# Last stage of a two-layer decoder: half tiles of 64 rows with up to two experts, expert weights laid out anew in DRAM

## The chip, the cores and the metric

The kernel runs on one NeuronCore of one Trainium2 chip. The metric is device time in microseconds, the median of three runs. TensorE (PE) multiplies matrices, VectorE (DVE), ScalarE (ACT) and GpSimd (POOL) do elementwise work, and DMA transfers are issued by SyncE (SP), ACT or POOL, each in its own order. All data are 32-bit floats.

## The reference, cut to what matters

The input x is 8 sequences of 256 tokens of 256 values, 2048 tokens in all. Two decoder layers follow each other, each with three parts that are added to x: layer 0 has self-attention, attention over a given memory `ctx_2048` and a feed-forward part with Sinkhorn routing; layer 1 has self-attention, attention over the same memory with one null key in front, and a mixture of eight experts, of which each token takes one, beside a shared expert that all tokens take. That last part is what the change is about (a = all 2048 tokens, D = 256, F = 704, E = 8; x is the layer-normed input):

```python
def _L1_ffn_ref(x_bsD, router_DE, w1_eDF, w3_eDF, w2_eFD, ws1_DF, ws3_DF, ws2_FD):
    x_aD = x_bsD.reshape(a, d)
    scores_aE = x_aD @ router_DE
    vals_aK, idx_aK = jax.lax.top_k(scores_aE, 1)
    masked_aE = jnp.full_like(scores_aE, -jnp.inf).at[jnp.arange(a)[:, None], idx_aK].set(vals_aK)
    gates_Ea = jax.nn.sigmoid(masked_aE).T
    routed_in_EaD = gates_Ea[:, :, None] * x_aD[None, :, :]
    mid_EaF = jax.nn.silu(einsum('ead,edf->eaf', routed_in_EaD, w1_eDF)) * einsum('ead,edf->eaf', routed_in_EaD, w3_eDF)
    routed_out_EaD = jnp.einsum('eaf,efd->ead', mid_EaF, w2_eFD)
    shared_aD = jax.nn.silu(x_aD @ ws1_DF) * (x_aD @ ws3_DF) @ ws2_FD
    out_aD = shared_aD + routed_out_EaD.sum(axis=0)
```

An expert's output for a token that did not choose it is zero, so the kernel computes each token with its own expert only.

## The kernel before, in words

`decoder` (L56) calls `plain` (L67), the usual path, and then tests `odd_i`: only where a check on the data failed does `general` compute everything again (L61 to L64). `plain` runs its stages in this order. Times are from the profiled execution.

- **Units of attention, 0 to about 600 us.** A loop (L739) goes over the units: self-attention of layer 0 and attention over the memory, two per sequence, then self-attention of layer 1. Each unit's `load()` is called two units ahead (L748); the memory keys and values (`memk` L424, `memv` L426) are loaded there on SP. At the second turn `expert_tables` (L491) prepares tables for layer 0's experts; it also fills the DRAM buffers `xs` and the end of `ys` with zeros, by DMAs from POOL (L496, L497). Layer 0's experts are woven in between.
- **The attention with a null key, about 600 to 1150 us** (`null_cross_attention`, L860), with two quarters of the shared expert at its end. `hidden` (L818) is the first half of a SwiGLU expert, `silu(x w1) * (x w3)`, for any number of columns; a `quarter` is `hidden` for 512 tokens.
- **The last stage, `token_experts` (L1072).** DVE works out from the router's scores which expert each token takes and its place in a list sorted by expert in which each expert begins at a new tile of 128 rows (L1117 to L1175), and which expert each tile has, `exp_i` (L1186). POOL scatters the 2048 scaled rows to these places in the DRAM buffer `xs`, in 16 indirect DMAs (L1195). Meanwhile TensorE does further shared work (`quarter(2)`, `joined`). Then come the tiles, `slots(0, 19)` (L1259, called at L1274), with an order of TensorE's instructions that is written out by hand: while tile t + 1 goes through `into`, tile t waits to go through `outof`, and tile t + 2 is `fetched`.
  - `fetched` (L1229), all on SP: the tile's 128 rows from `xs` into `xr` (four buffers; this DMA waits for all 16 scatters), a register load of the tile's expert, two DMAs for w1 and w3 side by side (`w_in`, L785, three buffers, and a copy of a tail of 64 columns by POOL, L790), two for w2 (`w_out`, L798). Then TensorE transposes the rows (L1243) and ACT copies them out of PSUM (L1245).
  - `into` (L1248): `hidden` for 128 rows, 22 matrix products written in the code, which the profile shows as 44 records `h` (L825); ACT does SiLU (L830), DVE the product (L831).
  - `outof` (L1254): six products written in the code, twelve records `out` (L1093), a copy by ACT (L1256) and a DMA by ACT's queue into `ye` (`ys` in the profile, L1257).
  - The list has room for 23 tiles. Registers of all engines load the number of filled tiles, and tiles 19 to 22 run only if it is above 19 (L1275 to L1279).
  - Then `quarter(3)` (L1285), 16 gathers by POOL from `ye` back to token order (L1288), DVE's additions, `joined(3)` and the output DMAs on SP (L1295 to L1302).

`product` splits a matrix product in two, each for 64 of the 128 rows of its output, which run side by side in the two halves of the array; the profile marks them 128*64, whole ones 128*128:

```python
def product(out, lhsT, rhs, start, stop):
    for h in (slice(0, 64), slice(64, P)):
        nc.tensor.matmul(out[h], lhsT[:, h], rhs, start=start, stop=stop, skip_group_check=True)
```

Outside the hand-written orders, a scheduler places each engine's instructions, DMA issues included, by when their inputs are ready and by program order.

Of the kernel before, what the change touches and what calls it, by code (L numbers as in the profile page):

```python
# [38 lines left out]
P = 128  # L39
# [11 lines left out]
SLOTS = NT + E - 1  # L51
NEG = -1.0e30
# [14 lines left out]
def plain(ctx: ExitStack, tc: tile.TileContext, a: dict, out: bass.AP, odd_i: bass.AP):  # L67
# [69 lines left out]

    xs = dram.tile([SLOTS * P, D], F32, name="xs")
    ye = dram.tile([SLOTS * P, D], F32, name="ys")

# [190 lines left out]
    class SelfAttention:  # L331
# [5 lines left out]
        def load(self):  # L337
            if self.layer == 0 and self.b > 1:
                load_x(self.b)

# [150 lines left out]
    def expert_tables():  # L491
# [4 lines left out]
        nc.gpsimd.dma_start(xs.rearrange("(s p) d -> p s d", p=P), zero.unsqueeze(1).to_broadcast([P, SLOTS, D]))  # L496
        nc.gpsimd.dma_start(  # L497
            ye[19 * P :].rearrange("(s p) d -> p s d", p=P), zero.unsqueeze(1).to_broadcast([P, SLOTS - 19, D])
        )

# [148 lines left out]
    def weights_x():  # L649
# [3 lines left out]
        ctxs = ctx.enter_context(tc.tile_pool(name="ctxs", bufs=2, side="right"))  # L653
        wproj = ExitStack()
        wp = wproj.enter_context(tc.tile_pool(name="wp", bufs=1, side="right"))
# [117 lines left out]
    fit = const.tile([P, B], F32, name="fit")  # L773

    w_l0.close()

# [41 lines left out]
    def hidden(mid, w13, cols, pair, silu):  # L818

        n = cols.shape[2]  # L820
        for i in range(NFC):
            h1, h3 = pair(n)
            for h, lo in ((h1, i * P), (h3, FF + tail + i * P))[: 2 if i < full else 1]:
                for c in range(2):
                    nc.tensor.matmul(h, w13[:, c, lo : lo + P], cols[:, c, :], start=c == 0, stop=c == 1)  # L825
            fw = P
            if i == full:
                fw, h1, h3 = tail, h1[:tail], h1[tail:]
            sl = silu(n)[:fw]
            nc.scalar.activation(sl, h1, AF.Silu)  # L830
            yield nc.vector.tensor_tensor(mid[:fw, i, :n], sl, h3, ALU.mult)  # L831

# [27 lines left out]
    def null_cross_attention(phase):  # L860
# [129 lines left out]

        def divide(oT, rs):
# [29 lines left out]
        def quarter(q):  # L1021
            return hidden(shared["mid_s"][q], shared["ws13"], shared["xnT"][:, :, bass.ts(q, 2 * S)], pair, silu)
# [8 lines left out]
        for b in range(B):  # L1031
# [13 lines left out]
            rs, old = reciprocals(b, den, en), en  # L1045
            if more:
# [25 lines left out]
    def token_experts(phase):  # L1072
        one = phase.enter_context(tc.tile_pool(name="e1", bufs=1))
        work = phase.enter_context(tc.tile_pool(name="e2", bufs=2))
        wts = phase.enter_context(tc.tile_pool(name="e3", bufs=3))
# [3 lines left out]
        xnT, ws13, ws2, mid_s = (shared[n] for n in ("xnT", "ws13", "ws2", "mid_s"))  # L1079

        mid_r = [ended(one.tile([P, NFC, P], F32, name=f"midr{i}")) for i in range(2)]
        w2_r = [ended(one.tile([P, NFC, D], F32, name=f"w2{i}")) for i in range(3)]
# [14 lines left out]
        def quarter(q):  # L1097
            mid = mid_s[q % 2]
            for last in hidden(mid, ws13, xnT[:, :, bass.ts(q, 512)], pair, silu):
                pass  # L1100
            return mid, last
# [8 lines left out]
        def row(n, step, name):  # L1110
            i = one.tile([P, n], I32, name=f"{name}_i")
            nc.gpsimd.iota(i, [[step, n]], base=0, channel_multiplier=0)
# [3 lines left out]

        ecol, tcol, jcol = row(E, -1, "ecol"), row(SLOTS, 1, "tcol"), row(NT, P, "jcol")  # L1117
        nc.vector.tensor_scalar(ecol, ecol, float(E), None, ALU.add)
# [28 lines left out]
        for j in range(NT):  # L1147
            nc.vector.tensor_tensor(run[:, j + 1, :], run[:, j, :], count[:, j, :], ALU.add)
        over = one.tile([P, E, NT], F32, name="overe")
        nc.vector.tensor_tensor(  # L1150
            over,
            run[:, NT, :].unsqueeze(2).to_broadcast([P, E, NT]),
            jcol.unsqueeze(1).to_broadcast([P, E, NT]),
            ALU.is_gt,
        )
        tiles = one.tile([P, E], F32, name="tiles")
        nc.vector.tensor_reduce(tiles, over, AX.X, ALU.add)
        at = one.tile([P, E + 1], F32, name="at")
        nc.vector.memset(at[:, 0:1], 0.0)
        for e in range(E):  # L1160
            nc.vector.tensor_tensor(at[:, e + 1 : e + 2], at[:, e : e + 1], tiles[:, e : e + 1], ALU.add)
        filled_i = one.tile([P, 1], I32, name="filled_i")
        nc.vector.tensor_copy(filled_i, at[:, E : E + 1])
        rows = one.tile([P, E], F32, name="rowse")
        nc.vector.tensor_scalar(rows, at[:, :E], float(P), None, ALU.mult)
        nc.vector.tensor_tensor(run[:, :NT, :], run[:, :NT, :], before, ALU.add)
        nc.vector.tensor_tensor(
            run[:, :NT, :], run[:, :NT, :], rows.unsqueeze(1).to_broadcast([P, NT, E]), ALU.add
        )
        nc.vector.tensor_tensor(run[:, :NT, :], run[:, :NT, :], hot, ALU.mult)  # L1170
        pos = one.tile([P, NT], F32, name="pos")
        nc.vector.tensor_reduce(pos, run[:, :NT, :], AX.X, ALU.add)
        nc.vector.tensor_scalar(pos, pos, SLOTS * P - 1.0, None, ALU.min)
        pos_i = one.tile([P, NT], I32, name="pos_i")
        nc.vector.tensor_copy(pos_i, pos)  # L1175
        past = one.tile([P, SLOTS, E - 1], F32, name="past")
        nc.vector.tensor_tensor(
            past,
            tcol.unsqueeze(2).to_broadcast([P, SLOTS, E - 1]),
            at[:, 1:E].unsqueeze(1).to_broadcast([P, SLOTS, E - 1]),  # L1180
            ALU.is_ge,
        )
        exp_f = one.tile([P, SLOTS], F32, name="exp_f")
        nc.vector.tensor_reduce(exp_f, past, AX.X, ALU.add)
        exp_i = one.tile([P, SLOTS], I32, name="exp_i")
# [20 lines left out]
        for q in range(3):  # L1206
# [6 lines left out]
            alld = dens.rearrange("p k t h -> p (k t h)")  # L1213
        inside = one.tile([P, 3 * NT * H], F32, name="inside")
# [1029 lines left out]
```

## Time and profile before

| | |
|---|---|
| median of three runs | 1417.25 us (1415.31 to 1417.82) |
| the profiled execution | 1415.5 us, its span 1413.4 us |
| TensorE busy | 1371.9 us, 97% of the span |
| DVE, ACT, POOL busy | 499.1, 461.9, 386.2 us |
| DMA over the span | 91.23 MB, mean 65 GB/s |
| granted clock of TensorE | 0.993 of full speed on average |
| the 19 tiles | 1226.55 to 1374.07 us |
| the test for further tiles, until TensorE goes on | 1374.07 to 1376.02 us |
| `quarter(3)` and `joined(3)` on TensorE | 1376.02 to 1405.5 us |
| last output DMA issued | 1406.57 us |

A line of the profile names the line of the code, the engine, the operation, the tiles it writes and reads, the form of a product in the array (rows * columns in use), partitions by elements, and the number of records, then busy time, the mean duration of one in ns, and the idle time of the engine just before, with what ended it. Products are pipelined: a record's duration is longer than the distance to the next one, so costs are read from start to start. In a timeline a line is a run of equal instructions: its start, its length, what it is. PEclk is the clock granted to TensorE, in parts of full speed. "DMA share" is the mean busy share of the 16 DMA engines.

### The profile page before, as it was taken

How to read it: one execution, taken by the hardware profiler on the slowest of the kernel's cores; microseconds unless marked ns; L12 is line 12 of the kernel's file. 1: busy time of each engine (PE TensorE's matmuls, PEld its weight loads, DVE VectorE, ACT ScalarE, POOL GpSimd, SP SyncE). 2: the span in 40 equal slices, each digit the busy share in tenths (PEclk: the TensorE clock that was granted, in tenths of full speed). 3: DMA queues.
4: the chain of work that ended last, by engine and by line, in shares of the span. 5: the costliest groups of instructions: out<-in, count | busy, mean ns of one | idle time of the engine just before them, and what ended most of it. 6: DMA issues, size and time to landing. Idle time of an engine off the chain costs nothing. (4 is left out here: it accounts for less than half of the span.)

```text
span 1413.4 us, 26349 instructions
## 1 busy us (share of the span) xinstructions
PE 1371.9 (97%) x10922; PEld 909.9 (64%) x10922; DVE 499.1 (35%) x1477; ACT 461.9 (33%) x754; POOL 386.2 (27%) x487
## 2 busy tenths in 40 slices
PE   6999999999999999999999999999999999999997
PEld 3666756756766666665565656565565646799984
DVE  6343553553555744420121313222121335222213
ACT  2555444444444344422221313222221311123221
POOL 4132142142043244212141414233141522200004
PEclk8999999999999999999999999999999999999999
DMA  9000000000000005010101011010101002588843
GB/s 314 20 13 16 16 16 9 16 16 1 2 9 2 2 8 218 1 63 16 31 16 46 17 31 31 16 32 16 31 2 31 16 16 75 208 304 315 306 164 122
DMA packets 54564, 91.23 MB, mean 65 GB/s; under 512 B 6160, under 2 KB 38720, under 8 KB 52896
## 3 DMA queue, kind: packets, MB, share of 16 engines
q1 hardware_dynamic: 47360, 70.00, 15.5%
q0 software_dynamic: 4064, 16.13, 3.1%
q10 hardware_dynamic: 3008, 3.28, 0.7%
q8 instruction: 90, 1.47, 0.4%
q14 instruction: 42, 0.34, 0.1%
HBM read 79.03 MB, written 10.37 MB: 63 GB/s over the span
## 5 line engine op out<-in xcount | busy, mean ns | idle before, releaser
L260 PE MATMUL o<-pT,padv 128*64 128x256 f32 (+1 forms) x1536 | 171.6, 366 | 1.2 <-POOL pT L240 1.2
L237 ACT ACTIVATE pT<-st 128x1024 f32<-128x1024 f32 (+1 forms) x128 | 110.6, 915 | 89.4 <-PE st L228 88.4
L260 PEld LDWEIGHTS o<-pT,padv 128*64 128x64 f32 x1536 | 103.1, 137 | 52.7 <-issue 10.1
L228 PE MATMUL st<-qm,kT 64*128 64x256 f32 (+1 forms) x1024 | 118.1, 370 | 1.4 <-DVE qm L206 1.4
L170 PE MATMUL fm<-ctxT,wkv_x 128*64 128x256 f32 x1024 | 112.9, 380 | 0.0
L170 PE MATMUL vps<-wkv_x,ctxT 128*64 128x512 f32 x512 | 111.8, 593 | 0.0
L228 PEld LDWEIGHTS st<-qm,kT 64*128 64x128 f32 x1024 | 91.1, 190 | 26.3 <-issue 15.1
L170 PEld LDWEIGHTS fm<-ctxT,wkv_x 128*64 128x64 f32 x1024 | 73.0, 137 | 37.3 <-issue 1.5
L825 PE MATMUL h<-xrT,w 128*128 128x128 f32 x836 | 96.6, 275 | 0.2 <-ACT xrT L1245 0.2
L923 POOL TENSOR_TENSOR both<-pTx 128x512 f32<-128x512 f32 x64 | 79.6, 1270 | 59.0 <-ACT pTx L921 34.0
L825 PEld LDWEIGHTS h<-xrT,w 128*128 128x128 f32 x836 | 94.9, 192 | 0.5 <-ACT xrT L1245 0.5
L921 ACT ACTIVATE pTx<-stx 128x1024 f32<-128x1024 f32 x64 | 62.0, 1021 | 90.0 <-PE stx L917 90.0
L170 PEld LDWEIGHTS vps<-wkv_x,ctxT 128*64 128x64 f32 x512 | 36.4, 137 | 68.9 <-issue 68.6
L237 ACT ACTIVATE pT<-st,kbias 128x1024 f32<-128x1024 f32 x64 | 68.0, 1112 | 28.8 <-PE st L228 28.7
L830 ACT ACTIVATE sl<-h 128x128 f32<-128x128 f32 (+1 forms) x126 | 38.6, 306 | 111.2 <-PE h L825 108.0
L152 POOL TENSOR_TENSOR lnrs<-lnve,mhalf 128x2 f32<-128x2 f32 x48 | 34.4, 723 | 146.8 <-DVE lnve L150 95.1
L831 DVE TENSOR_TENSOR midr<-sl,h 128x128 f32<-128x128 f32 x114 | 32.8, 288 | 109.9 <-ACT sl L830 61.1
L228 PE MATMUL st<-qm,memk 64*128 64x256 f32 x512 | 68.8, 393 | 0.5
L917 PE MATMUL stx<-qTx,kTx 64*128 64x256 f32 x512 | 64.3, 391 | 2.5 <-ACT pTx L921 2.5
L147 DVE BATCH_NORM_STATS2 lxst<-yx 128x6 f32<-128x256 f32 x16 | 6.0, 418 | 162.6 <-ACT yx L1005 162.6
L170 PE MATMUL qk<-l_wqkv,xnT 128*64 128x512 f32 x256 | 62.6, 610 | 0.7 <-ACT xnT L180 0.7
L240 POOL TENSOR_SCALAR_AFFINE_SELECT pT<-pT 128x512 f32<-128x512 f32 x64 | 39.5, 638 | 83.0 <-ACT pT L237 79.7
(260 smaller groups left out, 2091.3 us busy)
## 6 DMA issues: line engine op xcount, KB each, us to landing
w<-L_ffn_w_eDF SPq DMA_DIRECT2D x38, 704.0 KB
w<-L_ffn_w_eFD SPq DMA_DIRECT2D x19, 640.0 KB
rs<-rd SPq DMA_DIRECT2D x16, 512.0 KB
ctxT<-ctx_T SPq DMA_DIRECT2D x8, 512.0 KB
wkv_x<-L_xattn_Wkv POOLq DMA_DIRECT2D x1, 4096.0 KB, 17.1
xs<-zero POOLq DMA_DIRECT2D x1, 2944.0 KB, 15.7
xr<-xs SPq DMA_DIRECT2D x19, 128.0 KB
ys<-yr ACTq DMA_DIRECT2D x19, 128.0 KB
```

Source lines behind the costliest of these rows:

```text
L152: nc.gpsimd.tensor_tensor(rs[:, :n], ve[:, :n], mhalf[:, :n], ALU.pow)
L170: nc.tensor.matmul(out[h], lhsT[:, h], rhs, start=start, stop=stop, skip_group_check=True)
L228: nc.tensor.matmul(st[:, g, i, :n], kT[rows, c, bass.ts(kt, P)], qm[rows, 2 * mq + i, c, q0:], start=True, stop=True,)
L237: nc.scalar.activation(pT[:, :, :, :n], st[:, :, :, :n], AF.Exp, scale=scale, **kb)
L240: nc.gpsimd.affine_select(out=pT[:, :, :, :P], in_=pT[:, :, :, :P], compare_op=ALU.is_ge, fill=0.0, base=0, pattern=[[0, 2], [0, 2], [1, P ...
L260: nc.tensor.matmul(o[64 * i : 64 * i + 64, mq, q0:], v_pad[:, kt, 4 * c + 2 * mq + i, 2 * g : 2 * g + 2, :], pTs[kt][:, g, i, : S - q0], s ...
L825: nc.tensor.matmul(h, w13[:, c, lo : lo + P], cols[:, c, :], start=c == 0, stop=c == 1)
L830: nc.scalar.activation(sl, h1, AF.Silu)
L831: yield nc.vector.tensor_tensor(mid[:fw, i, :n], sl, h3, ALU.mult)
L917: nc.tensor.matmul(st[:, g, kt, :], kT[rows, c, bass.ts(kt, P)], qT[rows, c, :], start=True, stop=True)
L921: nc.scalar.activation(pT, st, AF.Exp, scale=scale)
L923: nc.gpsimd.tensor_tensor(both, pT[:, :, 0, :], pT[:, :, 1, :], ALU.add)
```

## The change

- **Half tiles.** The list of places is cut into halves of 64 rows. An expert begins at a new half. Whole pairs of halves of one expert come first; the odd halves that are left over from each expert come behind them and are paired with each other. The room is TILES = 20 tiles. Tiles 0 to 11 (PAIRED = 12) always have one expert; tiles 12 to 19 are computed as two halves with a weight set each, also where both halves have the same expert. `exp_i` has one entry for each of tiles 0 to 11 and two for each of the others. DVE's arithmetic for this is longer by about a dozen operations.
- **Products.** `into` uses `product` instead of whole products; in a tile with two sets it makes two of them, of 64 columns each. `outof` makes one product for each half of 64 rows, with the half's own w2.
- **Order.** 17 tiles run unconditionally, in a hand-written order that spreads the tiles with two sets among those with one. Rows of two tiles are transposed together. Tiles 17 to 19 run in a test at the very end, behind the whole output, with a buffer `yo` of their own, gathers and additions; `quarter(3)` follows the 17 tiles without a test.
- **Weights.** `pack(e)`, called with layer 1's units of self-attention, copies the weights of expert e from DRAM to a DRAM buffer `packs`, in five DMAs on SP, so that a partition's part of w1, w3 (with the tail in place) and of w2 lies in one piece each. A set is then loaded by two DMAs; POOL's tail copy is gone. There are four buffers for sets instead of three. In the built program the 40 copying DMAs stand on SP directly behind the loads of x and ahead of the loads of `memv` and `memk` of the last sequences.
- **Queues.** The rows of a tile are loaded by POOL's queue instead of SP's.
- **Also.** `expert_tables` fills `yo` and the unused ends in `packs` with zeros, nine more DMAs on POOL. The check of the denominators' range moves from the last stage to the attention with a null key (`in_range`).

The core of the diff:

```diff
+FIRST = 2 * FF
+TILES = NT + E // 2
+PAIRED = NT - E // 2
...
+    packs = dram.tile([E, P, 2 * FIRST + NFC * D], F32, name="packs")
+    def pack(e):
+        full, tail = FF // P, FF % P
+        to = packs[e, :, : 2 * FIRST].rearrange("p (c f) -> p c f", c=2)
+        w1, w3 = (a[f"L1_ffn_{n}_eDF"][e].rearrange("(c p) f -> p c f", p=P) for n in ("w1", "w3"))
+        nc.sync.dma_start(to[:, :, :FF], w1)
+        nc.sync.dma_start(to[:, :, FF : FF + tail], w3[:, :, full * P :])
+        nc.sync.dma_start(to[:, :, FF + tail :], w3[:, :, : full * P])
+        to, w2 = packs[e, :, 2 * FIRST :].rearrange("p (c d) -> p c d", d=D), a["L1_ffn_w2_eFD"][e]
+        nc.sync.dma_start(to[:, :full, :], w2[: full * P].rearrange("(c p) d -> p c d", p=P))
+        nc.sync.dma_start(to[:tail, full, :], w2[full * P :])
...
             if self.layer == 0 and self.b > 1:
                 load_x(self.b)
+            if self.layer == 1:
+                pack(self.b)
...
-        nc.gpsimd.dma_start(xs.rearrange("(s p) d -> p s d", p=P), zero.unsqueeze(1).to_broadcast([P, SLOTS, D]))
+        nc.gpsimd.dma_start(xs.rearrange("(s p) d -> p s d", p=P), zero.unsqueeze(1).to_broadcast([P, TILES, D]))
         nc.gpsimd.dma_start(
-            ye[19 * P :].rearrange("(s p) d -> p s d", p=P), zero.unsqueeze(1).to_broadcast([P, SLOTS - 19, D])
+            ye[17 * P :].rearrange("(s p) d -> p s d", p=P), zero.unsqueeze(1).to_broadcast([P, TILES - 17, D])
         )
+        nc.gpsimd.dma_start(yo.rearrange("(s p) d -> p s d", p=P), zero.unsqueeze(1).to_broadcast([P, TILES - 16, D]))
+        for e in range(E):
+            nc.gpsimd.dma_start(packs[e, FF % P :, 2 * FIRST + FF // P * D :], zero[FF % P :])
...
-    def hidden(mid, w13, cols, pair, silu):
-        n = cols.shape[2]
+    def hidden(mid, first, n, pair, silu):
         for i in range(NFC):
             h1, h3 = pair(n)
             for h, lo in ((h1, i * P), (h3, FF + tail + i * P))[: 2 if i < full else 1]:
-                for c in range(2):
-                    nc.tensor.matmul(h, w13[:, c, lo : lo + P], cols[:, c, :], start=c == 0, stop=c == 1)
+                first(h, lo)
...
+        begin = one.tile([P, 2, E], F32, name="begin")
+        nc.vector.tensor_scalar(begin[:, 0, :], full_at[:, :E], 2.0, None, ALU.mult)
+        nc.vector.tensor_tensor(begin[:, 1, :], all_at[:, :E], full_at[:, :E], ALU.subtract)
+        nc.vector.tensor_scalar(begin[:, 1, :], begin[:, 1, :], filled[:, 0:1], None, ALU.add)
...
+        n = PAIRED + 2 * (TILES - PAIRED)
+        past = one.tile([P, n, 2, E - 1], F32, name="past")
+        for k in range(2):
+            nc.vector.tensor_tensor(
+                past[:, :, k, :],
+                tcol.unsqueeze(2).to_broadcast([P, n, E - 1]),
+                begin[:, k, 1:].unsqueeze(1).to_broadcast([P, n, E - 1]),
+                ALU.is_ge,
+            )
+        exp_f = one.tile([P, n], F32, name="exp_f")
+        nc.vector.tensor_reduce(exp_f, past.rearrange("p n k e -> p n (k e)"), AX.X, ALU.add)
+        nc.vector.tensor_scalar(tcol, tcol, filled[:, 0:1], None, ALU.is_ge)
+        nc.vector.scalar_tensor_tensor(exp_f, tcol, 1.0 - E, exp_f, ALU.mult, ALU.add)
...
-        def fetched(t):
+        nc.vector.tensor_scalar(odd_i, fine, P - 0.5, None, ALU.is_lt)
+        def rows(t):
             xr = work.tile([P, D], F32, tag="xr", name="xr", bufs=4)
-            get = nc.sync.dma_start(xr, xs[bass.ts(t, P), :])
+            get = nc.gpsimd.dma_start(xr, xs[bass.ts(t, P), :])
             for put in puts:
                 tc.add_manual_dep(get.ins, put.ins.name, landed, reason="a tile's rows come from any token")
-            e = nc.sync.value_load(exp_i[0:1, t : t + 1], min_val=0, max_val=E - 1)
-            def of(n):
-                return a[f"L1_ffn_{n}"][bass.ds(e, 1), :, :].rearrange("a p d -> (a p) d")
-            w13 = w_in(wts, of("w1_eDF"), of("w3_eDF"), "w13")
-            w2 = w_out(w2_r[t % 3], of("w2_eFD"))
+            return xr
+        def fetched(t):
+            sets = []
+            for i in [t] if t < PAIRED else [2 * t - PAIRED, 2 * t - PAIRED + 1]:
+                e = nc.sync.value_load(exp_i[0:1, i : i + 1], min_val=0, max_val=E - 1)
+                of = packs[bass.ds(e, 1), :, :].rearrange("a p d -> (a p) d")
+                w13 = wts.tile([P, 2, FIRST], F32, tag="w13", name="w13")
+                nc.sync.dma_start(w13.rearrange("p c f -> p (c f)"), of[:, : 2 * FIRST])
+                w2 = wts.tile([P, NFC, D], F32, tag="w2", name="w2")
+                nc.sync.dma_start(w2.rearrange("p c d -> p (c d)"), of[:, 2 * FIRST :])
+                sets.append((w13, w2))
+            return sets
+        def turned(tiles):
             ps = mm.tile([P, 2, 2 * P], F32, tag="mm", name="xrp")
-            for c in range(2):
-                nc.tensor.transpose(ps[:, c, :P], xr[:, bass.ts(c, P)], ident)
-            xrT = work.tile([P, 2, P], F32, tag="xrT", name="xrT", bufs=3)
-            nc.scalar.copy(xrT, ps[:, :, :P])
-            return w13, w2, xrT
-        def into(t, w13, w2, xrT):
-            mid = mid_r[t % 2]
-            for _ in hidden(mid, w13, xrT, pair, silu):
+            n = P * len(tiles)
+            for i, xr in enumerate(tiles):
+                for c in range(2):
+                    nc.tensor.transpose(ps[:, c, bass.ts(i, P)], xr[:, bass.ts(c, P)], ident)
+            xrT = work.tile([P, 2, 2 * P], F32, tag="xrT", name="xrT")
+            nc.scalar.copy(xrT[:, :, :n], ps[:, :, :n])
+            return [xrT[:, :, bass.ts(i, P)] for i in range(len(tiles))]
+        def into(t, sets, xrT):
+            mid_r.append(mid_r.pop(0))
+            mid, n = mid_r[-1], P // len(sets)
+            def first(h, lo):
+                for i, (w13, _) in enumerate(sets):
+                    for c in range(2):
+                        product(h[:, bass.ts(i, n)], w13[:, c, lo : lo + P], xrT[:, c, bass.ts(i, n)], c == 0, c == 1)
+            for _ in hidden(mid, first, P, pair, silu):
                 pass
-            return mid, w2
-        def outof(t, mid, w2):
+            return mid, sets
+        def outof(t, mid, sets):
+            ps = mm.tile([P, 2 * D], F32, tag="mm", name="out")[:, :D]
+            for i in range(NFC):
+                for k, h in enumerate((slice(0, 64), slice(64, P))):
+                    nc.tensor.matmul(
+                        ps[h],
+                        mid[:, i, h],
+                        sets[k % len(sets)][1][:, i, :],
+                        start=i == 0,
+                        stop=i == NFC - 1,
+                        skip_group_check=True,
+                    )
             yr = work.tile([P, D], F32, tag="yr", name="yr")
-            nc.scalar.copy(yr, outward(mid, w2, 0))
-            nc.scalar.dma_start(ye[bass.ts(t, P), :], yr)
-        def slots(lo, hi):
-            with tc.manual_schedule(engines={mybir.EngineType.PE}):
-                got = {lo: fetched(lo), lo + 1: fetched(lo + 1)}
-                ahead = into(lo, *got.pop(lo))
-                for t in range(lo, hi):
-                    now = ahead
-                    if t + 2 < hi:
-                        got[t + 2] = fetched(t + 2)
-                    if t + 1 < hi:
-                        ahead = into(t + 1, *got.pop(t + 1))
-                    outof(t, *now)
-        slots(0, 19)
-        filled = nc.values_load(filled_i[0:1, 0:1], min_val=NT, max_val=SLOTS)
-        with tc.If(filled > 19):
-            slots(19, 21)
-            with tc.If(filled > 21):
-                slots(21, SLOTS)
+            nc.scalar.copy(yr, ps)
+            nc.scalar.dma_start(ye[bass.ts(t, P), :] if t < 17 else yo[bass.ts(t - 16, P), :], yr)
+        def slots(order):
+            n = len(order)
+            xr = [rows(t) for t in order[:2]]
+            got, xrT = [fetched(t) for t in order[:2]], turned(xr)
+            xr = [rows(t) for t in order[2:4]]
+            ahead = into(order[0], got.pop(0), xrT.pop(0))
+            for i, t in enumerate(order):
+                now = ahead
+                if i + 2 < n:
+                    got.append(fetched(order[i + 2]))
+                    if i % 2 == 0:
+                        xrT += turned(xr)
+                        xr = [rows(t) for t in order[i + 4 : i + 6]]
+                if i + 1 < n:
+                    ahead = into(order[i + 1], got.pop(0), xrT.pop(0))
+                outof(t, *now)
+        with tc.manual_schedule(engines={mybir.EngineType.PE}):
+            slots([0, 1, 12, 2, 3, 13, 4, 5, 14, 6, 7, 15, 8, 9, 16, 10, 11])
 
         ov = out.rearrange("b (t p) d -> (b t) p d", p=P)
 
 
 
-        mid, last = quarter(3)
+        with tc.manual_schedule(engines={mybir.EngineType.PE}):
+            mid, last = quarter(3)
         places = [*range(12, NT), *range(12)]
         for j in places:
             nc.gpsimd.indirect_dma_start(
@@ -1300,6 +1402,27 @@
                         nc.sync.dma_start(ov[j], x[:, j, :])
                 joined(3, mid, i)
                 nc.sync.dma_start(ov[12 + i], x[:, 12 + i, :])
+        more = nc.values_load(filled_i[0:1, 0:1], min_val=2 * NT, max_val=2 * TILES - 1)
...
+        with tc.If(more > 34):
+            with tc.manual_schedule(engines={mybir.EngineType.PE}):
+                slots([17])
+                with tc.If(more > 36):
+                    slots([18, 19])
```

## The prediction

> **What bounds the kernel now.** I read the page first: the engines' shares, then the forty slices, then the groups.
>
> ```profile
> PE 1371.9 (97%) x10922; PEld 909.9 (64%) x10922; DVE 499.1 (35%) x1477; ACT 461.9 (33%) x754; POOL 386.2 (27%) x487
> ...
> L825 PE MATMUL h<-xrT,w 128*128 128x128 f32 x836 | 96.6, 275 | 0.2 <-ACT xrT L1245 0.2
> ```
>
> TensorE is busy for 97% of the span, so a saving has to remove matrix products or TensorE idle time. The second line is the first half of the routed experts: 836 records = 19 tiles of 44. Its 0.2 us of idle says that nothing keeps TensorE waiting there. Next I asked for the windows of the last stage, and for one stretch much earlier, where the large weight `wkv_x` is loaded:
>
> ```profile
> 1250.00:1275.00 25.00, 25.00 (x193) 23.93 (x192) 5.76 (x20) 7.46 (x26) 0.88 (x3) 1.00 0.91 315
> 1325.00:1350.00 25.00, 25.00 (x192) 23.85 (x191) 5.47 (x19) 7.83 (x27) 0.88 (x3) 1.00 0.85 293
> ```
> ```profile
> 546.00:552.00 6.00, 6.00 (x56) 3.69 (x52) 3.63 (x7) 2.15 (x6) 5.36 (x8) 1.00 1.02 423
> ```
>
> After the stretch come its length, then busy time by engine (PE first), and last granted clock, DMA share and GB/s. TensorE is full at clock 1.00, but the DMA engines are already at 0.85 to 0.91 of their time with only 293 to 325 GB/s moved; with 8 KB rows the same engines moved 423. The timeline gives one tile's period:
>
> ```profile
> 1340.82 5.08 PE L825 MATMUL h<-xrT,w 128*128 128x128 f32 x44
> 1345.73 2.76 PE L1093 MATMUL out<-w,midr 128*128 128x256 f32 x12
> 1348.33 0.38 PE L1243 MATMUL xrp<-ident,xr 128*128 128x128 f32 x2
> 1348.54 5.08 PE L825 MATMUL h<-xrT,w 128*128 128x128 f32 x44
> ```
>
> From start to start: 4.91 us for 44 products (112 ns each), 2.60 for 12 (217 ns each), 0.21 for two transposes: 7.72 us a tile. The 19 tiles run from 1226.55 to 1374.07, 147.5 us. So the stage is paid by the tile, and each tile costs the same whether its 128 rows are full or not.
>
> **The tiles.** The reference's inputs route 325, 377, 367, 187, 190, 249, 168 and 185 tokens to the eight experts. In tiles of 128 for one expert that is 19. In halves of 64 it is 34, exactly 17 tiles: 12 with one weight set in a fixed place, five (places 12 to 16) always computed as two halves with two sets each. `more > 34` is false, so the late tiles do not run.
>
> *A tile with one set.* Each product becomes two of 64 output columns side by side. The trace prices this form: `v` L170 at 39.76 has four pairs of halves of 256 columns, 215 ns a pair, against 217 for a whole one in `out`. So 44 x 110 + 12 x 217 = 4.84 + 2.60 = 7.44 us, times 12 = 89.3.
>
> *A tile with two sets.* 88 pairs with 64 moving columns each. Before has no product with 64 columns. The nearest rows are short ones, bursts of 16 halves (8 pairs) with 8 columns:
>
> ```profile
> 139.62 0.64 PE L170 MATMUL lg<-gate,xnT 128*64 128x8 f32 x16
> 140.11 1.93 PE L260 MATMUL o<-pT,padv 128*64 128x256 f32 x16
> ...
> 146.26 0.59 PE L170 MATMUL lg<-gate,xnT 128*64 128x8 f32 x16
> 146.70 1.93 PE L260 MATMUL o<-pT,padv 128*64 128x256 f32 x16
> ```
>
> Start to start they take 0.49 and 0.44 us, 61 and 55 ns a pair[...]. Half of the 110 ns of 128 columns is 55. I take 62. Lower end 55; upper end 110, as if 64 columns saved nothing. The Trainium skill ("TensorE: Matmul & The Clock Gate", Back-to-back issue gap) gives about 60 cycles for 1 to 64 columns, with an issue floor near 25 ns, but 62 ns per product when hardware decoding is off. At 62 a product, a pair would be 124 ns and the five tiles 5 x 88 x 0.062 = 27 us dearer, which turns the change into a loss. The rows of 55 to 61 ns a pair exclude it for eight pairs in a row; for 88 no row does. So 88 x 62 + 12 x 217 = 5.46 + 2.60 = 8.06 us, times 5 = 40.3.
>
> *Around them.* Transposes 17 x 0.22 = 3.7. They stay whole products, two tiles at a time, so the array changes form 18 times; one change costs about 0.09 us (the first `o` after a `tr` comes 202 ns after it, against 109): 1.7. Sum 89.3 + 40.3 + 3.7 + 1.7 = 135.0, with the same 0.8 for the first fill 135.8, against 147.5: **-11.7 us**.
>
> **Does DMA keep up?** 17 tiles take 22 sets of 2.23 MB (w13 11,264 and w2 6,144 bytes on each of 128 partitions) instead of 19 of 2.16. In the steady order (two single tiles, one double) TensorE needs 2 x 7.44 + 8.06 + 0.9 = 23.9 us for three tiles, and DMA has to bring 4 x 2.23 MB and move 3 x 0.26 MB of rows, 9.7 MB: 23.1 us at 420 GB/s, 24.9 at 390, 27 at 360. It is nearly balanced. Before's 293 to 325 GB/s in 0.85 to 0.91 of the time come with rows of 1 and 2.8 KB; sets from `packs` have rows of 6 and 11 KB, nearest to the 8 KB of the 423 row. Skill and row differ here: "DMA: Bandwidth & Descriptors", Measured, gives a core about 358 GB/s when both cores of the memory domain stream, and some 425 alone. At 358 a set takes 6.2 us instead of 5.3 and, the shortfall is 27 - 23.9 = 3.1 us in each of 5.7 groups of three tiles, 17 us, less the lead of a set or so that four buffers hold (6 us): about 10 us; at 420 about none, at 390 about 4. One core runs here and the 423 was its own, so I take 410 to 420 and **+1 us**; ends 0 and +10.
>
> A help is at the stage's head. SP's queue in before:
>
> ```profile
> 1196.24 0.42 SPq L789 DMA_DIRECT2D w<-L_ffn_w_eDF  x1
> 1215.59 0.82 SPq L1231 DMA_DIRECT2D xr<-xs  x2
> 1216.61 0.39 SPq L799 DMA_DIRECT2D w<-L_ffn_w_eFD  x1
> ```
>
> The first row load waits for the scattered rows to land and holds w2 of tile 1 and all behind it for 19 us. In the change the row loads wait on POOL instead; behind them there is nothing but the next rows. SP loads four sets (8.9 MB, 22 us) from about 1195, ready before 1226. The routing chain on DVE gets about a dozen small operations longer (0.15 to 0.3 us each, +2 us), so the puts end near 1216 and land by 1222: 4 us of cover.
>
> **The branch behind the stage.**
>
> ```profile
> 1374.07 0.37 ACT L1256 COPY yr<-out 128x256 f32<-128x256 f32 x1 [2.22 <-PE out L1093]
> ...
> 1376.02 3.27 PE L825 MATMUL h<-xnTe,ws 128*128 128x512 f32 x7 [1.99 <-ACTq L1276]
> ...
> 1377.22 1.01 POOL L1288 DMA_INDIRECT xg<-ys,pos_i  x1 [18.71 <-SPq L1276]
> ```
>
> TensorE waits 1.99 us for the test of `filled`; now quarter(3) follows at once: **-2.0**. The 16 gathers (1.25 us each) start about 3 us after the stage and land some 26 after it; the tail of quarter(3) takes 29.5: hidden, with 3 us left. The test moves to the very end, ahead of the last odd-case test, where nothing covers it: 0 to +3, I take **+1.5**.
>
> **Laying out the weights.** 40 transfers from DRAM to DRAM on SP, 17.3 MB read and written. The program order puts all of them right behind the loads of x, from about 30 us, and ahead of `memv` of the fourth batch (after 27 of them) and `memk` (after all). In before these were issued at 68.9 and 83.3 but used at 154.0 and 155.7; `memv` of the third is used at 132.6. So the copies have until about 150 us: 140 GB/s suffice. No row of the trace has such a transfer. The same page, in its table of measured facts, has 207 to 214 GB/s for copies within DRAM in rows of 16 KB (82 us here, done at 112); rows here are 256 bytes to 2.8 KB, so I count on less. I take 0; if the rate were 100, they would end at about 203 and TensorE would stand for some 47 us. On POOL, nine more fills stand behind the first ones (0.8 us each, 7 us, but issue may wait for earlier fills to land, 13 to 16 us each):
>
> ```profile
> 34.42 1.28 POOL L356 TENSOR_TENSOR qc<-qc,turned 128x512 f32<-128x512 f32 x1 [9.61 <-DVE qc L307]
> ```
>
> The 9.6 us of idle absorb them only in part; this product then ends 2 to 6 us later, and TensorE wants what comes of it at 44.37. Ends 0 and +6, I take **+1**. The range check moved to DVE early in the null attention (six operations of 0.4 us, under an engine 35% busy): 0.
>
> **Sum.** -11.7 - 2.0 + 1.0 + 1.5 + 1.0 = -10.2. In the profiled execution: 1415.5 (span 1413.4) to 1405.3. The median of the runs lies 1.75 us above that execution, so I put the same step to it: 1417.25 - 10.2 = **1407**.
>
> **The rivals.**
> *A, transfers take over.* If sets come at 360 to 385 GB/s, or a set's landing lags its issue by 3 us, TensorE waits at the double tiles: +4 to +10, 1410 to 1417. For: DMA already 0.91 busy; four buffers. Against: long rows, and the 423.
> *B, slower than before: many small products.* A double tile issues twice the weight loads and products of a single one in nearly the same time. If 88 pairs in a row cost not 62 ns but p, the five tiles lose 440 x (p - 62) ns. The gain is gone at p = 85 (440 x 23 ns = 10.2 us); at p = 110 it is 21 us: 1428. For: the densest long stretch of before, 200 instructions in 7.8 us (39 ns each), is far from the 15 ns needed. Against: the bursts at 55 to 61.
> *C, the copies or fills at the start hold layer 0*: 1420 to 1455.
> *D, it does not do what it says*: tokens not packed as counted, so the late tiles run behind everything, about 30 us: 1437. The counts speak against it.
> *E, better*: p = 53, no wait at start or end, 1415.5 - 17 in the profile: 1399 to 1401.
>
> **Chances.** Forecast (1402 to 1410) 0.58, E 0.09, A 0.20, B 0.07, C 0.04, D 0.02. Within 0.2% (2.8 us, about what a measurement here tells from no change) lies the upper end of A: 0.04. Faster 0.58 + 0.09 + 0.16 = 0.83; slower 0.07 + 0.04 + 0.02 = 0.13. The range 1399 to 1417 covers the forecast, E and A and leaves out B, C and D.
>
> **What would show it.** Right: the stage takes 134 to 138 us with TensorE full in each 25 us window, DMA near 0.95 at 390 to 420 GB/s; double tiles are 0.6 us longer than single ones; quarter(3) starts without a gap. Wrong: idle before a double tile's first product released by a DMA (A); `h` pairs above 85 ns (B); TensorE idle near 44, 133 or 155 us (C); products of the stage behind quarter(3) (D).

## The result and the profile after

The change takes 1408.43 us in the median of five runs (1406.11 to 1409.93) against 1417.25: a ratio of 0.9937, 95% interval 0.9923 to 0.9952, or 8.8 us less. Two repetitions gave 0.9949 (0.9935 to 0.9963) and 0.9943 (0.9929 to 0.9956). 1407 was forecast. The sum came out nearly right, but by luck: two of its terms were wrong by 4 to 5 us each, and they cancelled.

The page of the changed kernel, in the order in which before's was read (busy time and count; then busy us, mean ns, and the idle time ahead of the group with its releaser):

```profile
span 1404.3 us, 28691 instructions
...
PE 1357.4 (97%) x12198; PEld 884.7 (63%) x12198; DVE 498.5 (35%) x1484; ACT 457.0 (33%) x730; POOL 395.1 (28%) x493
...
L191 PE MATMUL h<-xrT,w 128*64 128x128 f32 (+1 forms) x1936 | 88.9, 253 | 5.1 <-DMA w<-packs 4.5
```

The share of TensorE is still 97% and does not show the change. The last line does: the `h` products of the tiles, which had 0.2 us of idle time, now have 5.1, and a weight transfer ends 4.5 of it. The windows of the stage show where (TensorE's busy time first, last the clock, DMA share and GB/s):

```profile
1250.00:1275.00 25.00, 23.83 (x439) 20.64 (x437) 5.44 (x19) 6.57 (x22) 1.06 (x2) 1.00 0.97 381
1275.00:1300.00 25.00, 22.81 (x384) 19.26 (x382) 4.07 (x15) 6.24 (x20) 2.07 (x4) 0.93 0.94 365
1300.00:1325.00 25.00, 25.00 (x466) 21.97 (x464) 5.76 (x20) 7.14 (x24) 0.60 (x2) 1.00 0.95 383
1325.00:1350.00 25.00, 23.89 (x434) 20.33 (x432) 5.18 (x18) 6.95 (x23) 0.00 (x0) 1.00 1.00 393
```

DMA is nearly full, as forecast, but moves 365 to 393 GB/s and not 410 to 420, and TensorE is full in only one of the four windows. The timeline of TensorE shows three kinds of tiles:

```profile
1237.84 5.30 PE L191 MATMUL h<-xrT,w 128*64 128x64 f32 x176
1242.97 2.76 PE L1347 MATMUL out<-w,midr 128*64 128x256 f32 x24
...
1279.04 5.03 PE L191 MATMUL h<-xrT,w 128*64 128x128 f32 x88
1283.89 2.76 PE L1347 MATMUL out<-w,midr 128*64 128x256 f32 x24
1286.48 0.40 PE L191 MATMUL h<-xrT,w 128*64 128x64 f32 x8
1289.07 6.67 PE L191 MATMUL h<-xrT,w 128*64 128x64 f32 x168 [2.19 <-DMA w<-packs]
```

The first pair is a tile with two sets that found them loaded: 5.13 us from start to start for 88 pairs (58 ns each) and 2.6 for `out`. A tile with one set takes 4.85 and 2.6. The last two lines are a double tile that did its first eight products with its first set and then waited for the second. From start to start its other products take 6.5 us; in the double tile before, they took 4.95 (1263.41 to 1268.36). The clock had fallen, as a view below shows.

| part, profiled execution | before | after | difference | forecast |
|---|---|---|---|---|
| start to the stage's first transposes | 1226.55 | 1223.52 | -3.0 | +1.0 |
| the stage, to the end of its last `out` | 147.5 | 141.3 | -6.2 | -11.7 + 1.0 |
| from there to quarter(3) | 2.0 | 0.0 | -2.0 | -2.0 |
| quarter(3) to the end of the span | 37.4 | 39.6 | +2.2 | +1.5 |
| span | 1413.4 | 1404.3 | -9.1 | -10.2 |

### The profile page after: what moved, and what is told of

Its sections match the earlier page's. It is cut to its first block, busy times and chain, and to the rows that moved or that the text cites. A ratio compares the mean times of both kernels' runs of the same rounds, so it can differ in the third digit from the quotient of the medians.

```text
span 1404.3 us, 28691 instructions
## 1 busy us (share of the span) xinstructions
PE 1357.4 (97%) x12198; PEld 884.7 (63%) x12198; DVE 498.5 (35%) x1484; ACT 457.0 (33%) x730; POOL 395.1 (28%) x493
## 4 chain that ended last, share of the span: by engine, by line
PE 80%; DMA 7%; DVE 5%; POOL 4%; issue 1%; ACT 1%; SPq 1%; ACTq 0%; POOLq 0%; DVEq 0%
PE fm L191 12%; PE st L249 8%; PE o L281 8%; PE vps L191 8%; PE h L191 5%; PE wo L191 4%; PE ox L992 4%; PE stx L954 4%; PE out L1141 3%; PE h L864 3%; PE out L1347 3%; PE qk L191 2%; DMA packs<-L_ffn_w_eDF 2%; PE tr L198 2%; PE hx L864 2%; PE den L968 2%
## 5 line engine op out<-in xcount | busy, mean ns | idle before, releaser
L191 PEld LDWEIGHTS fm<-ctxT,wkv_x 128*64 128x64 f32 x1024 | 73.0, 137 | 37.3 <-issue 1.3
L191 PE MATMUL h<-xrT,w 128*64 128x128 f32 (+1 forms) x1936 | 88.9, 253 | 5.1 <-DMA w<-packs 4.5
L191 PEld LDWEIGHTS h<-xrT,w 128*64 128x64 f32 x1936 | 85.9, 140 | 8.4 <-DMA w<-packs 4.9
L856 ACT ACTIVATE sl<-h 128x128 f32<-128x128 f32 (+1 forms) x114 | 35.3, 310 | 108.8 <-PE h L191 59.6
L857 DVE TENSOR_TENSOR midr<-sl,h 128x128 f32<-128x128 f32 x102 | 29.4, 288 | 107.3 <-PE h L191 74.4
L261 POOL TENSOR_SCALAR_AFFINE_SELECT pT<-pT 128x512 f32<-128x512 f32 x64 | 39.6, 640 | 83.0 <-ACT pT L258 79.7
```

The lines of the kernel that those rows point to most:

```text
L261: nc.gpsimd.affine_select(out=pT[:, :, :, :P], in_=pT[:, :, :, :P], compare_op=ALU.is_ge, fill=0.0, base=0, pattern=[[0, 2], [0, 2], [1, P ...
```

## The experiments

Three groups, each on one chip, each timed against before on the same chip. On the first group's chip every profile has TensorE standing some 4 to 7 us near 1210 us while POOL issues the scatters, and before's median is 1422.7; totals of that group are compared only with each other. The totals expected for experiments 1 to 4 were all missed by 7 us and more: in these four the stage begins 8 to 13 us later than in the first profile of the change. My theory (Q) for the stage was the order on SP, the rival (W) the bandwidth. SP's queue in the changed kernel (L1313 issues w13, L1315 w2):

```profile
1271.71 0.34 SPq L1313 DMA_DIRECT2D w<-packs  x1
1278.54 0.33 SPq L1315 DMA_DIRECT2D w<-packs  x1
1279.08 0.33 SPq L1313 DMA_DIRECT2D w<-packs  x1
1279.67 0.33 SPq L1315 DMA_DIRECT2D w<-packs  x1
1280.20 0.81 SPq L1313 DMA_DIRECT2D w<-packs  x1
1286.69 0.33 SPq L1315 DMA_DIRECT2D w<-packs  x1
```

A w2 stands 6.8 us behind its w13 (1271.7 to 1278.5) and is issued when an `out` has ended (the one that began at 1275.76): it takes the buffer that this `out` reads, that of tile 13's first set, four sets earlier. The next w13 stands behind it, although the `into` that used its buffer (1263.41 to 1268.53) was long over. Then three transfers are issued in 1.2 us and share the rate with the one before them. In the chain of waits (start, us) that w13 takes

```profile
1279.08 9.95 DMA w<-packs
```

9.95 us to land, and it is the one for which TensorE waits until 1289.07.

The main waits of SP for buffers, 1195 to 1375 us (what waited for what: us in total, times, the longest; first the change, then experiment 1, where L1320 issues w13 and L1312 w2):

```profile
SPq L1315 <- PE out L1347: 60.6, 9, 8.3
SPq L1313 <- PE xrp L1325: 5.9, 1, 5.9
```
```profile
SPq L1320 <- PE h L191: 38.1, 9, 5.7
SPq L1312 <- PE out L1355: 37.3, 9, 7.1
```

In the change no w13 is seen to wait for the `h` products that use its buffer: the w2 ahead of it has waited longer. In experiment 1 nine of them do, and are issued as soon as their own buffer is free.

**1, order.** In `fetched`, w2 of the set before is issued behind w13. `second()` issues the one that was put off; where nothing is left to fetch, it is called alone. The main lines:

```diff
                 nc.sync.dma_start(w13.rearrange("p c f -> p (c f)"), of[:, : 2 * FIRST])
+                second()
                 w2 = wts.tile([P, NFC, D], F32, tag="w2", name="w2")
-                nc.sync.dma_start(w2.rearrange("p c d -> p (c d)"), of[:, 2 * FIRST :])
+                late.append((w2, of))
```

> Each set's w2 is issued behind the w13 of the next set instead of ahead of it; same bytes, same buffers. Theory Q (SP's order: a w2 that waits for the output products of the tile four sets earlier holds the next w13, whose buffer is already free, so the DMA engines stand idle for 2 to 4 us a time): the three stalls of 1.2 to 2.4 us ahead of double tiles and the clock dip behind the second one (1.6 us) go, the stage falls from 141.2 to about 135 us, total about 1402 (1408.4 - 5 to 6.5). Theory W (bandwidth: 9.7 MB for every 24 us of TensorE is simply too much): stalls unchanged within 1 us, total 1407 to 1410.

The stage took 136.9 us, with no wait for a weight in it; experiment 3, with the change's order on the same chip, took 145.3. Q holds, W falls: same bytes, same buffers. (136.9 is 2 us above the 135 expected; 0.9 and 0.4 of it are gaps that the profile lays to nothing.) Two windows of this kernel, whose stage begins 13 us later:

```profile
1275.00:1300.00 25.00, 25.00 (x454) 21.37 (x452) 5.20 (x18) 7.24 (x24) 2.13 (x4) 1.00 1.00 403
1300.00:1325.00 25.00, 24.56 (x446) 20.75 (x442) 5.20 (x18) 7.06 (x24) 1.51 (x3) 1.00 1.00 404
```

In these windows DMA has no gap left, and TensorE hardly any.

**2, one set for both halves.**

```diff
-            for i in [t] if t < PAIRED else [2 * t - PAIRED, 2 * t - PAIRED + 1]:
+            for i in [t] if t < PAIRED else [2 * t - PAIRED]:
...
-            return sets
+            return sets if t < PAIRED else 2 * sets
```

> The five double tiles load only one set and use it for both halves; the second half's weights are left out, so 17 sets instead of 22. TensorE's products are the same in number and shape. Both Q and W: no stall, TensorE full throughout the stage, clock 1.00, stage 133.5 to 135 us (12 x 7.40 + 5 x 7.73 + transposes 5 + 1), total about 1402. If the stage stays above 138, the double tiles cost TensorE something that is no wait for weights.

Stage 135.7 us, no wait for a weight, 1416.39 us against 1416.97 of experiment 1. So 136 us is what TensorE needs, and order alone recovers all but a microsecond. The prediction's figure for the stage without waits, 135.8, was right; the 133.5 to 135 expected here was a little low.

**3, no test at the end.** `more` and its block (L1408 to L1425) left out.

> The test at the very end and what stands in it are left out: tiles beyond 17 are never computed. Theory: the tail from the first product of quarter(3) to the end of the span, 39.5 us after the change against 37.3 before, falls back to about 37.3, because POOL's closing work (1.5 us and a drain of 5.4 us, begun only behind the test) starts earlier; total about 1406.2. Rival: POOL's closing work starts when the gathers are done anyway and the test costs under 0.5 us: total 1408.

From the last output DMA's issue to the end of the span: 5.6 us, against 9.1 in experiment 2 and 8.1 in experiment 1. The tail from the first product of quarter(3) is 42.0 us, and not 37.3 as expected, since TensorE and SP's output DMAs have waits in it on this chip; with the test it is 44.9 in experiments 1 and 2. By either count the test costs 2.5 to 3.5 us. The reason expected holds: in the change POOL's closing work of 1.5 and 5.4 us begins at 1396.6, behind the test, and ends 0.8 us ahead of the span's end; here it begins at 1405.7, 11 us ahead of the last output DMA, and is not the last thing. The total, 1419.86 us, says nothing alone, since the change itself did not run on this chip.

**4 and 10, without the layout.**

```diff
-                of = packs[bass.ds(e, 1), :, :].rearrange("a p d -> (a p) d")
...
+                w13 = w_in(wts, of("w1_eDF"), of("w3_eDF"), "w13")
+                w2_r.append(w2_r.pop(0))
+                sets.append((w13, w_out(w2_r[-1], of("w2_eFD"))))
```

> The change without the layout: no copies, no fills for them, sets loaded from the original weights by four DMAs with rows of 2.8 and 1 KB and a tail copy on POOL. Half tiles, order and queues as in the change. If the long rows pay: a set takes 3.6 us at 402 GB/s and 2.0 us at 356, 5.6 instead of 5.3 us, and twice the issues; with the waits in SP's order stalls rise from 5 us to 8 to 14, total 1410 to 1418. If the rows do not matter: total 1407 (the POOL wait of 1.4 us at 44 us goes).

Stage 143.4, total 1425.15 us, 5.3 above experiment 3, of which some 3 are the test that 3 lacks, so 2 to 3 us remain for the layout. Its waits for weights come to 5.9 us, not the 8 to 14 expected. That left open whether the layout pays, so it ran again beside the change:

> The change without the layout, as in the fourth experiment, on another chip: original weights by four DMAs a set with rows of 2.8 and 1 KB. If long rows are worth what their rate says (5.3 against 5.6 us a set and a second issue), 2 to 6 us above the change. If they are worth nothing, within 1 us of it: in the fourth experiment the stage took 143.4 us, no more than the change's own 141.3 to 145.3.

1413.11 against 1408.04 of the change in the same group: 5.1 us, and the stage 147.6 against 142.2. So the layout is worth 2 to 5 us. In this profile 2.6 of the stage's 5.4 us are a slower clock behind waits: two dips of 1.6 and 2.6 us against one of 1.6 in the change. Experiment 4's profile has no dip in its stage.

**5, before again.** One profile on the second group's chip.

> The kernel before, once more, for a profile on the same chip as the other three of this group. On the chip of the first four experiments TensorE stood for about 7 us near 1208 us, in the scatters, in all of them, and the clock fell to 0.5 behind it; no profile of before exists from that chip. If that wait belongs to the chip, it is here too, at the scatters; if the change's faster loading of four sets brings it, before has none.

No wait in the scatters here, nor in the change on this chip; so no profile shows before on the first group's chip, and the question stays open. It showed something else, the row behind the test:

```profile
1375.41 20.85 PE L825 MATMUL h<-xnTe,ws 128*128 128x512 f32 x44 [1.99 <-ACTq L1276]
```

In the first profile of before the same 44 products took 19.15 us. The window 1376 to 1378 has a clock of 0.50: a wait of 2 us in the test can be followed by 1.7 us more of slow products, as in one of the two profiles of before.

**6, the change again,** and as the anchor of the third group.

> The change, once more, on the chip of this group: against before as measured first, ratio 0.9937 (about -9 us); if the wait in the scatters belongs to the change and to the chip, only -2 to -5 us here. Stage 141 to 145 us with three or four waits for w<-packs.

> The change once more, as the anchor of this group: ratio to before 0.994 to 0.995, stage 141 to 143 us.

1408.38 and 1408.04 us; stages 142.6 and 142.2, four waits for `w<-packs` each, 5.4 and 5.2 us together.

**7, all three edits.** Order as in 1; one test (below) and no late tiles; the unused ends of `packs` copied by SP instead of filled by POOL.

```diff
+        nc.vector.tensor_scalar(odd_f[:, 0:1], fine, P - 0.5, None, ALU.is_lt)
+        nc.vector.tensor_scalar(odd_f[:, 1:2], filled[:, 1:2], 34.5, None, ALU.is_gt)
+        nc.vector.tensor_reduce(odd_i, odd_f, AX.X, ALU.max)
```

> Three edits to the change: w13 of the next set ahead of w2 (as in the first experiment); the tests for late tiles and for odd data joined into one, so that tokens beyond 17 tiles take the general path and the end has one test; no fills on POOL, the unused ends are copied from w2's first rows by SP. Theory: -5 to -6.5 (stalls and clock dip), -2.3 (second test), -1 (POOL's wait at 44 us): 8 to 10 us below the change on the same chip, ratio to before near 0.987. Rival (the stage is bound by bandwidth, the end by POOL's drain): under 3 us below the change.

1400.01 us, 8.4 below the change on the same chip, ratio to before 0.9887 (0.9872 to 0.9902). It is the fastest version here and still covers every routing, since more than 34 halves go to `general`. In the profiles the stage is 136.9 against 142.6 us and the end 6.4 against 9.1: -5.7 and -2.7. The stage begins 0.7 later, so that taking the fills off POOL shows no gain, and the spans differ by 7.6. The w13 that came late in the change, issued at 1279.08, stands here at

```profile
1271.55 0.33 SPq L1319 DMA_DIRECT2D w<-packs  x1
```

though both stages begin at 1223.5. Its windows:

```profile
1250.00:1275.00 25.00, 25.00 (x466) 21.95 (x462) 5.77 (x20) 7.02 (x25) 1.07 (x2) 1.00 1.00 398
1275.00:1300.00 25.00, 24.54 (x436) 20.66 (x433) 5.19 (x18) 7.04 (x23) 2.13 (x4) 1.00 1.01 404
```

TensorE is full here but for 0.46 us that the profile lays to no other engine or transfer; another such gap, of 0.97 us, lies ahead of these windows. DMA is full too: the two are at least as closely balanced as the forecast's 23.9 against 23.1 us.

**8, fills alone.**

```diff
-        for e in range(E):
-            nc.gpsimd.dma_start(packs[e, FF % P :, 2 * FIRST + FF // P * D :], zero[FF % P :])
...
+        nc.sync.dma_start(to[tail:, full, :], w2[: P - tail])
```

> The change with only the fills of packs taken off POOL (the unused ends are copied by SP from w2's first rows). Theory: the 1.40 us in which TensorE waits at 44 us for qkr are gone, total 1.0 to 1.4 us below the change; rival: other work fills that wait anyway and the total stays within 0.5 us.

1408.05 against 1408.38 us, with runs from 1403.6 to 1412.1: not to be told apart. The wait at 44 us is gone from the trace all the same (1.51 us in the change on this chip). Inconclusive for the total. Its stage took 139.5 us, with the change's own order: its longest wait for a weight is 1.76 us, and no slow clock follows.

**9, before without its test.** The test behind the 19 tiles (L1275 to L1279) left out; tiles 19 to 22 are never computed.

> The kernel before without the test behind the 19 tiles; tiles 19 to 22 are never computed. Theory: TensorE's wait of 1.99 us ahead of quarter(3) goes and nothing takes its place: 2.0 us below before, ratio 0.9986. Rival: the gathers, which start with the end of the test, then become the last thing and take back more than half: ratio 0.9993 or above.

1410.13 us, ratio to before 0.9953 (0.9939 to 0.9967): 6.4 us, at least 4.7. Both expectations missed. In its profile quarter(3) starts without a gap (2.0), its products take 19.05 us and not the 20.85 that before can have (up to 1.8), and the end, 5.4 us from the last output DMA, is 1.4 shorter than before's 6.8. That is up to 5.2; the rest is not traced.

**11, the best version without the layout.**

> The better version of the second group (w13 ahead of the previous w2, one test, no fills) without the layout: loads from the original weights, no copies. Four sets and three tiles' rows take 4 x 5.6 + 2.1 = 24.5 us against 23.6 us of TensorE for three tiles, so DMA just bounds the stage: 3 to 6 us above the better version's ratio of 0.9887, so 0.991 to 0.993. Rival (order was all, rows do not matter): 0.989 as with the layout.

1405.05 us, ratio 0.9913 (0.9899 to 0.9926), by the ratios 3 to 4 us above the version with the layout, which ran on another chip. Stage 142.0: one wait of 2.1 us for a weight with a clock dip behind it, and 2.4 us of gaps with no releaser. In these profiles rows and order each give 5 to 6 us in the stage, clock dips included.

## Why the prediction held, point by point

**Tiles: right.** A single tile at 7.45 us (7.44 forecast; its 110 ns a product stood against 112 in the line shown, and 110 came out), a double one at 7.73 (8.06): 88 pairs of 64 columns in a row run at 58 ns, as the bursts with 8 columns had said. Rival B falls. The stage without waits is 135.7 to 136.9 us (135.8).

**DMA: the step that failed.** "At 420 about none", taken as +1 us, was wrong by about 5 us. The three waits of double tiles (1.17, 2.19 and 1.11 us) and the slow products behind the second (1.6) are 6.1 us, and 141.3 less 6.1 is 135.2; the new order alone took the stage to 136.9. The rate was a little under the 410 to 420 assumed, but it sufficed: with no gap left, the windows above of experiments 1 and 7 move 398 to 404 GB/s, and at 404 the 9.7 MB of three tiles take 24.0 us (an estimate) beside TensorE's 23.9. (The sum was not consistent either: at 390 GB/s it falls short by 1.0 us in each of 5.7 groups, less than the 6 us of lead that it takes off at 358, so it gives about nothing there and not 4.) What I mis-sized is when the transfers start. I compared bytes with TensorE's time and took the buffers as the only limit; I did not follow what stands behind a waiting transfer on SP, which the view of before's queue had shown me once already (`xr` ahead of w2). Each w2 waits for an `out` and holds the next w13. By the signs named ahead this part failed: the stage lies outside 134 to 138 us, and TensorE waits for DMA in double tiles. It is rival A in its effect, by another mechanism than its rate of 360 to 385 GB/s. The counts ahead also show bytes to save: they make 15 whole pairs of halves and 4 odd ones, so three of the five double tiles load one expert's set twice, 6.7 MB. Leaving that out was not tried.

**The clock: not in the sum.** Behind the wait that begins at 1286.9 us the change has

```profile
1286.00:1290.00 4.00, 1.81 (x35) 1.48 (x32) 0.00 (x0) 0.65 (x2) 0.00 (x0) 0.91 1.01 418
1290.00:1292.00 2.00, 2.00 (x44) 2.00 (x41) 0.29 (x1) 0.28 (x1) 0.00 (x0) 0.50 0.97 405
```

half the clock for some 3 us: 1.6 us lost beyond the wait. In the stages of all profiles, single waits for a weight of up to 1.90 us (experiment 3) drew no dip, and those of 2.08 us and more did; two waits of 1.14 us with 0.7 us between them did in experiment 10, as did 1.87 and 1.34 us there, but two of 1.32 and 1.18 us in experiment 4 did not. The Trainium skill ("TensorE: Matmul & The Clock Gate", Part 1: The HAM clock gate) says that the clock halves after an idle window of about 3.4 us, that the window runs freely, and elsewhere on the page that gaps above about 3 us are to be avoided. By that no wait of the change would cost more than itself; by the rows, one of 2.19 us did.

**The start: wrong by 4.** The forecast was +1 and the trace gave -3.0. POOL's fills did make TensorE wait for `qkr` (1.40 us at 44 us, none in before), as said. All the same, the change is 0.3 us ahead at 49 us. Both have half the clock behind waits near 20 us, in before until 31 us, in the change only until 27, and the `qk` products behind it start at 29.64 instead of 31.60. In the five profiles without any of the new fills (before twice, experiments 7, 9 and 11) they start at 31.55 to 31.88, in the nine others at 28.75 to 30.21. So the fills may have paid for themselves; how was not tried.

Most of the rest comes later. In before a wait of 2.60 us for `qkr` is followed by a slow clock, in the change a wait of 2.56 us is not (windows 202 to 204 us, before first):

```profile
202.00:204.00 2.00, 2.00 (x17) 1.25 (x19) 0.75 (x1) 0.58 (x1) 0.00 (x0) 0.50 0.00 0
```
```profile
202.00:204.00 2.00, 2.00 (x36) 1.12 (x34) 1.07 (x2) 1.01 (x2) 0.00 (x0) 1.00 0.00 0
```

That is 1.6 us. The same wait one unit later (2.66 us at 308 in before, 2.56 at 306 in the change) is followed by the slow clock in both. Over all 14 profiles the wait near 202 us has 2.3 to 2.7 us, and 7 of them dip there, with and without the copies; so it is not shown that the change removes it, and the gain is luck as far as is known. Another 0.5 us is a shorter wait ahead of `counts` at 1176 us (0.61 against 1.16): the range check that left DVE's chain there is the likely reason, not tried alone. The last 0.5 us comes in small steps between 210 and 600 us.

**The tests: right in the trace, too small in the runs.** -2.0 was read off the gap; experiment 9 puts the whole price of a test in the middle at 4.7 to 8.6 us. The one at the end cost +2.2 in the profile and 2.5 to 3.5 between kernels with and without it, at the upper end of my 0 to +3 or above it. Moving the test was worth less than removing it.

**The copies: right.** Hidden: done by 92 us, 41 us before the first `memv` behind them was used in before. They moved 17.3 MB in about 60 us (30 to 91), some 280 GB/s beside other loads, with rows of 256 bytes to 2.8 KB. The 207 to 214 GB/s that the Trainium skill ("DMA: Bandwidth & Descriptors", Latency and other measured facts) has for copies with rows of 16 KB, from which I expected less, is too low here. Rival C falls, and D: 17 tiles ran, no more.

**The gathers: right.** POOL has issued the last by 1388.5 us, and no `out` of the tail waits for them.

## What to carry to other kernels

Whether transfers keep up is a question of bytes and of gaps: for each transfer in an in-order queue, ask which consumer's end it waits for and what ready transfer stands behind it, and issue first what becomes ready first. A conditional block can cost more than the gap that it shows (here 6.4 us against 2.0), in part since half the clock can follow a wait of 2 us; fold rare cases into a test that is there already. Products with 64 moving columns in half the array hold their price over a whole tile (58 ns a pair), so padding to tiles can be cut finely where weights come in time.

## What was not expected of the hardware

The clock dip behind waits of 2.0 to 2.7 us, in half of the profiles for one and the same wait. Copies within DRAM at some 280 GB/s with short rows. On one chip, waits of 4 to 7 us near 1210 us, in which ACT and DVE both stood though the products that they wait for had been issued; in experiment 2 both went on at 1214.3, 2.7 us after POOL's last scatter had been issued. Two other chips had none in the change itself, and the cause stays open.
